# Cross-attention scores laid out by key: chunk maxima on VectorE, turned and spread as equal columns on TensorE

## The chip, the cores and the metric

The kernel runs on one core of a Trainium2 chip. The metric is the device time of one execution in microseconds (us). Before the change it is 1261.9 us, the median of three runs (1261.23, 1261.9, 1263.66). All operands are float32.

The engines are named as the profile names them: PE is TensorE's matmul stream and PEld its weight loads, DVE is VectorE, ACT is ScalarE, POOL is GpSimd, SP is SyncE, which only issues DMAs.

## The reference

One decoder layer on `x` (32 batches, 112 queries, 256 features) with a context of 375 keys in each batch: windowed self-attention, cross-attention, and a mixture of 8 experts (two for each token), each behind a layer norm and added to `x`. The change touches the cross-attention alone (16 heads of 16 features):

```
q = (hidden_states @ Wq).reshape(B, S, H, D).transpose(0, 2, 1, 3)
kv = (key_value_states @ Wkv).reshape(B, K, 2, H, D)
...
scores = jnp.einsum('bhsd,bhkd->bhsk', q, k)
rel = jnp.arange(K)[None, :] - jnp.arange(S)[:, None]
bias = rel_bias[_relative_position_bucket(rel)].transpose(2, 0, 1)[None]
scores = scores + bias
attn = jax.nn.softmax(scores, axis=-1)
out = jnp.einsum('bhsk,bhkd->bshd', attn, v).reshape(B, S, E)
return out @ Wo
```

A softmax over 375 keys thus needs, for each of 112 queries and 16 heads, the largest score, the exponentials of what lies below it, their sum, and the product with `v`. The sum comes out of that product: `v` carries a column of ones.

## The kernel before

**Slots.** The attention part is a list of slots, written out by hand and walked in the loop at L1226. A slot handles four heads (one in each 32-row strip of PE's array) of one batch: a cross item (g, b, s), from slot 20 to slot 147, and a self item two groups ahead, up to slot 119. Slots 0 to 18 hold self items only. Batches come in 8 groups of 4, so a group's cross items fill 16 slots. PE, DVE and ACT run in exactly the order in which the loop issues their instructions (`tc.manual_schedule(engines=IN_ORDER)`), and `pool_order` (L121) ties POOL's instructions to the same order.

**One slot.** The loop issues, in this order:

1. `scores` (L464). PE writes four banks `sc`, one for each strip: cross scores with queries on 112 partitions and 375 keys along the row (L477), and beside them self scores (L488). For each strip DVE adds the bias (or the mask), negates, stores `w`, and finds the row's least (L503, one instruction with its accumulator read). POOL then takes the least off `w` (L509): 4 x 375 elements for cross, 4 x 112 for self.
2. `average` (L533), in every second slot, for items three and four slots back: PE multiplies weights with `v` (L554), ACT copies the result (L558).
3. `weigh` (L515) for the item of two slots back: PE transposes `w` chunk by chunk, three chunks of 125 keys for cross and one of 112 for self, four heads each (L530), and ACT takes the exponential of each chunk into `wT`, with keys on the partitions (L531). Two of the chunks stand first, the others between the steps of 4.
4. Steps of the slot: projections of queries, keys and values (L383, L416, L450), context loads (L434), transposes of normed rows (L377).
5. Late steps: `divide` (L562), `turn` (L580), `attended` (L589) with its residual adds on DVE (L602), statistics of the layer norms (L343, L344), routing (L623 to L718), with small steps that go from DVE to POOL and back (L643 to L650, L676 to L678).

PE's order matters: the next slot's `scores` stand behind all of this slot's work on PE. The four `sc` banks serve one slot, so the next slot's cross scores wait for L503 on the bank. The transposes of `weigh` wait for POOL's L509, two slots earlier.

**The bias** (L288) is a table with queries on 112 partitions, all heads and 375 keys, spread by one DMA from a table by relative position (L298). The keys of the context come reversed from the host, so that the position runs the same way along both.

**After the attention** the expert part takes over (L1061): it starts while the last slots run, and is bound by PE and DMA. Its code isn't touched.

Of the kernel before, what the change touches and what calls it, by code (L numbers as in the profile page):

```python
# [11 lines left out]
F32 = mybir.dt.float32  # L12
# [26 lines left out]
NWARM = 24  # L39
LAG = 4  # L40
# [10 lines left out]
IN_ORDER = {mybir.EngineType.PE, mybir.EngineType.DVE, mybir.EngineType.Activation}  # L51
# [27 lines left out]
def decoder_kernel(  # L79
# [95 lines left out]
    with ExitStack() as att, ExitStack() as own_att:  # L175
# [112 lines left out]
        bias = wpool.tile([S, H, K], F32, name="bias")  # L288

        def spread_bias():  # L290

            vps = ps_pj.tile([P, 512], F32, tag="pj", name="vps")
            nc.tensor.matmul(vps[:H, :NREL], rb, hot, start=True, stop=True)
            by_rel = two.tile([H, NREL], F32, tag="ct", name="by_rel")
            nc.vector.tensor_copy(by_rel, vps[:H, :NREL])
            by_rel_d = dram.tile([H, NREL], F32, name="by_rel_d")
            nc.sync.dma_start(by_rel_d, by_rel)
            nc.sync.dma_start(  # L298
                bias,
                bass.AP(  # L300
                    tensor=by_rel_d.tensor, offset=by_rel_d.offset,
                    ap=[[1, S], [NREL, H], [1, K]],
                ),
            )
# [120 lines left out]
        def cross_queries(g, c):  # L425
            if c == 0:
                cross_q[g] = two.tile([P, NC2, 2, GT], F32, tag="q_cross", name=f"q_cross{g}")
            ps = ps_pj.tile([P, GT], F32, tag="pj", name=f"q2ps{g}_{c}")
            project(ps, wq_sb[:, :, c * P:(c + 1) * P], normed[g, 2][1])
            by_parity(cross_q[g][:, c], ps, g == 0)  # L430
# [32 lines left out]

        def scores(cross, selfs):  # L464

            name = "_".join(str(v) for part in (cross or (), *selfs) for v in part)
            w = two.tile([S, 4, K + S], F32, tag="w", name=f"w{name}", bufs=3)
            low = small.tile([S, 3, 4], F32, tag="low", name=f"low{name}")
            at = K if cross else 0
            sc = [ps_sc.tile([S, 512], F32, tag="sc", name=f"sc{name}_{r}") for r in range(4)]  # L470
            if cross:
                g, b, s = cross
                c, p = divmod(s, 2)
                kT, q = keys[g, b][1], cross_q[g]
                for r in range(4):
                    rows = slice(32 * r, 32 * r + 32)
                    scored[cross] = nc.tensor.matmul(  # L477
                        sc[r][:, :K], q[rows, c, p, b * S:(b + 1) * S], kT[rows, c, :],
                        start=True, stop=True,
                    ).ins  # L480
            if selfs:
                g, b, s = selfs[0]
                c, p = divmod(s, 2)
                n, at_b = len(selfs), slice(b * S, (b + 1) * S)
                q, k = self_in[g, c]
                for r in range(4):
                    rows = slice(32 * r, 32 * r + 32)
                    nc.tensor.matmul(  # L488
                        sc[r][:, at:at + n * S].rearrange("q (p k) -> q p k", p=n),
                        q[rows, at_b], k[rows, p:p + n, at_b], start=True, stop=True,  # L490
                    )
            spans = []
            if cross:
                spans.append((0, K))
            spans += [(at + i * S, at + (i + 1) * S) for i in range(len(selfs))]
            for r in range(4):
                for i, (lo, hi) in enumerate(spans):
                    if cross and i == 0:
                        c, p = divmod(cross[2], 2)
                        add = bias[:, 8 * c + 2 * r + p, :]  # L500
                    else:
                        add = wmask
                    nc.vector.tensor_tensor_reduce(  # L503
                        out=w[:, r, lo:hi], in0=sc[r][:, lo:hi], in1=add,
                        scale=-1.0, scalar=FAR, op0=ALU.add, op1=ALU.min,
                        accum_out=low[:, i, r:r + 1],
                    )
            for i, (lo, hi) in enumerate(spans):
                nc.gpsimd.tensor_tensor(  # L509
                    w[:, :, lo:hi], w[:, :, lo:hi],  # L510
                    low[:, i].unsqueeze(2).to_broadcast([S, 4, hi - lo]), op=ALU.subtract,
                )
            return w

        def weigh(cross, selfs, j, w):  # L515

            n = NKC if cross else 0
            if j == 0:
                name = "_".join(str(v) for part in (cross or (), *selfs) for v in part)
                wT = two.tile([KC, NKC + 1, 4, S], F32, tag="wT", name=f"wT{name}", bufs=3)  # L520
                if cross:
                    turned["c", *cross] = wT, 0
                for i, part in enumerate(selfs):
                    turned["s", *part] = wT, n + i
            wT, _ = turned[("c", *cross) if cross else ("s", *selfs[0])]
            lo, m = (j * KC, KC) if j < n else (n * KC + (j - n) * S, S)
            kind = "c" if j < n else "s"
            tp = ps_tr.tile([KC, 4, S], F32, tag="tr", name=f"{kind}tr{wT.name}_{j}")
            for r in range(4):
                nc.tensor.transpose(tp[:m, r, :], w[:, r, lo:lo + m], ident[:S, :S])  # L530
            nc.scalar.activation(wT[:m, j], tp[:m], AF.Exp, scale=-1.0)  # L531

        def average(half, cross, own):  # L533
# [9 lines left out]
            for i, (k, (g, b)) in enumerate(sides):  # L543
                for p in range(2):
                    wT, first = turned.pop((k, g, b, 2 * half + p))
                    n = NKC if k == "c" else 1
                    for j in range(n):
                        for r in range(4):
                            h = 8 * half + 2 * r + p
                            if k == "c":  # L550
                                v, x = v_cross[b % 2][:, j, h, :], wT[:, j, r, :]
                            else:
                                v, x = v_self[:, b, h, :], wT[:S, first, r, :]
                            nc.tensor.matmul(  # L554
                                av[32 * r:32 * r + 32, i, p, :], v, x,
                                start=(j == 0), stop=(j == n - 1),
                            )
# [660 lines left out]
        with tc.manual_schedule(engines=IN_ORDER):  # L1218
# [7 lines left out]
            for slot in range(min(steps), max(steps) + 1):  # L1226
# [12 lines left out]
                if slot in plan_at:  # L1239
                    planning = plan_at[slot]()  # L1240
                if slot in items:
                    made[slot] = scores(*items[slot])
                parts = []
                if slot - 2 in items:
                    cross, selfs = items[slot - 2]
                    w = made.pop(slot - 2)
                    n = NKC * bool(cross) + len(selfs)
                    parts = [partial(weigh, cross, selfs, j, w) for j in range(n)]
# [3 lines left out]
                for half in range(2):  # L1252
                    if sides := averages.get((slot, half)):
                        do(partial(average, half, sides.get("c"), sides.get("s")))
                for part in parts[:2]:
# [69 lines left out]
```

## Time and profile before

| what | value |
|---|---|
| median of three runs | 1261.9 us |
| the profiled execution | 1270.7 us, span 1269.0 us |
| self-attention slots alone | 0 to 84.8 us |
| cross and self slots (24 to 119) | about 105 to 739 us |
| cross slots alone (120 to 147) | 739 to 884 us |
| passage to the experts, experts | 884 to 1269 us |

How to read it: the page gives busy times of each engine, and the chain of work that ended last. Matmuls are pipelined, so the busy time of PE says little about its pace; the distance between the starts of two instructions of one kind says more. A row of groups has the line, the engine, the operation, what it writes and reads with shapes, the number of instructions, and after the bar the busy time with the mean of one in ns, then the engine's idle time just before them with what ended it. In a table by stage the columns after the stage are its length, the busy time and number of instructions of PE, PEld, DVE, ACT and POOL, PE's granted clock, the DMA engines' share and GB/s. In a list of waits the numbers are us in total, times, and the longest. In a timeline they are the start and the length in us, with the number of records merged; a float32 matmul leaves two records, a transpose one.

### The profile page before, as it was taken

Reading aid. Unit: us, or ns where it says so; the run is one execution under the profiler, and the core shown is the slowest. Engines: PE = TensorE matmul, PEld = TensorE weight load, DVE = VectorE, ACT = ScalarE, POOL = GpSimd, SP = SyncE. Lnnn points to the kernel's source line nnn. Section 1 sums busy time; section 2 is a strip of 40 time slices with the busy share of each in tenths; the row PEclk is TensorE's granted clock in tenths of the full one; section 3 lists DMA queues with packets and bytes.
Section 4 is the critical chain, followed back from the end, with each engine's and each line's share of the span. In section 5 each row is a group of like instructions: output and inputs, shape, how many; then the busy total and the mean of one; then the engine's idle time right before and its main releaser. Section 6 shows DMA issues by size and latency. Waiting matters only on the chain.

```text
span 1269.0 us, 29648 instructions
## 1 busy us (share of the span) xinstructions
PE 1227.4 (97%) x11648; PEld 972.5 (77%) x11648; DVE 651.0 (51%) x3012; ACT 570.1 (45%) x1201; POOL 839.0 (66%) x784
## 2 busy tenths in 40 slices
PE   9999999999999999999999999998789999999997
PEld 6666776777787787778778777766678898888886
DVE  5653654665566566557566665665325323332221
ACT  4454554555556456555555545454222222222222
POOL 8545664577767777767776796687556655665552
PEclk9999999999999999999999999999889999999999
DMA  8129876731100200200110020130366778888882
GB/s 229 34 69 197 203 169 161 180 87 42 44 26 14 73 14 14 74 24 15 39 33 26 14 59 26 36 128 25 115 209 195 212 208 276 239 234 244 244 247 30
DMA packets 70204, 143.00 MB, mean 113 GB/s; under 512 B 5521, under 2 KB 60498, under 8 KB 65074
## 3 DMA queue, kind: packets, MB, share of 16 engines
q0 software_dynamic: 20784, 85.92, 23.1%
q1 hardware_dynamic: 49282, 55.20, 17.3%
q8 instruction: 92, 1.51, 0.5%
q14 instruction: 46, 0.38, 0.1%
HBM read 90.88 MB, written 50.21 MB: 111 GB/s over the span
## 4 chain that ended last, share of the span: by engine, by line
PE 92%; ACT 2%; DVE 2%; POOL 1%; issue 1%; another core or an unknown queue 1%; DMA 0%; POOLq 0%; ACTq 0%; DVEq 0%
PE gu L1018 18%; PE wT L530 14%; PE py L1037 9%; PE sc L477 8%; PE k2ps L383 6%; PE v2ps L450 6%; PE avc_s L554 6%; PE ops L597 4%; PE ctrwT L530 3%; PE sc L488 3%; PE vps L416 2%; PE qps L383 2%; PE q2ps L383 2%; PE kps L383 2%; PE tp L377 1%; ACT wT L531 1%
## 5 line engine op out<-in xcount | busy, mean ns | idle before, releaser
L509 POOL TENSOR_TENSOR w<-w,low 112x448 f32<-112x448 f32 (+1 forms) x256 | 459.4, 1814 | 211.1 <-DVE low L503 210.1
L503 DVE CUSTOM_DVE_ANT_0 w<-sc,bias 112x375 f32<-112x375 f32 x512 | 270.4, 542 | 118.2 <-PE sc L488 96.2
L531 ACT ACTIVATE wT<-wT 125x448 f32<-125x448 f32 (+1 forms) x394 | 199.0, 542 | 100.7 <-PE wT L530 94.3
L1018 PE MATMUL gu<-xT,w 128*128 128x256 f32 (+1 forms) x1248 | 229.9, 342 | 1.9 <-issue 1.9
L530 PEld LDWEIGHTS wT<-ident,w 112*125 112x125 f32 (+1 forms) x1576 | 187.6, 174 | 46.1 <-issue 14.2
L1018 PEld LDWEIGHTS gu<-xT,w 128*128 128x128 f32 x1248 | 202.1, 192 | 26.8 <-issue 5.7
L530 PE MATMUL wT<-ident,w 112*125 112x112 f32 (+1 forms) x1576 | 216.0, 275 | 5.8 <-ACT wT L531 5.8
L1026 DVE SCALAR_TENSOR_TENSOR hid<-gu,w,sil 128x256 f32<-128x256 f32 (+1 forms) x156 | 67.2, 432 | 233.6 <-ACT sil L1023 228.2
L1044 POOL DMA_INDIRECT out_dram<-y,to x63 | 100.4, 1594 | 111.8 <-ACT y L1043 94.2
L1023 ACT ACTIVATE sil<-gu,w 128x256 f32<-128x256 f32 (+1 forms) x156 | 67.5, 433 | 147.4 <-PE gu L1018 131.9
L503 DVE CUSTOM_DVE_ANT_0 w<-sc,wmask 112x112 f32<-112x112 f32 x512 | 129.0, 268 | 2.6 <-PE sc L488 2.6
L477 PE MATMUL sc<-kT,q_cross 32*112 32x375 f32 x1024 | 123.3, 518 | 1.3 <-DVE low L503 1.0
L1037 PE MATMUL py<-w,hid 128*128 128x256 f32 x504 | 116.8, 383 | 0.4 <-DVE x L767 0.4
L1037 PEld LDWEIGHTS py<-w,hid 128*128 128x128 f32 x504 | 94.0, 193 | 12.1 <-DVE x L767 0.6
L450 PE MATMUL v2ps<-wkv_sb,ct 128*125 128x256 f32 x384 | 94.3, 381 | 0.0
L383 PE MATMUL k2ps<-ct,wkv_sb 128*128 128x375 f32 x256 | 92.3, 483 | 0.0
L503 DVE DVE_READ_ACCUMULATOR2_ANT low<- 112x1 f32 x1024 | 84.0, 82 | 0.0
L602 DVE TENSOR_TENSOR x<-x,ops 112x256 f32<-112x256 f32 x64 | 24.8, 418 | 111.1 <-PE ops L597 110.9
L1043 ACT ACTIVATE y<-py,gate 128x256 f32<-128x256 f32 x63 | 27.2, 471 | 108.6 <-PE py L1037 106.8
L725 POOL DMA_INDIRECT xslots<-xn,to x64 | 61.8, 966 | 19.7 <-issue 14.8
L962 POOL DMA_INDIRECT xg<-xslots,rows_i x63 | 60.7, 963 | 18.9 <-issue 17.4
L450 PEld LDWEIGHTS v2ps<-wkv_sb,ct 128*125 128x125 f32 x384 | 67.2, 188 | 7.7 <-DVE q_cross L389 0.5
(208 smaller groups left out, 1646.6 us busy)
## 6 DMA issues: line engine op xcount, KB each, us to landing
xslots<-zeros SPq DMA_DIRECT2D x28, 1060.0 KB, 7.6
ct<-in_ctx_t_dram SPq DMA_DIRECT2D x32, 375.0 KB, 3.3
x<-in_x_dram SPq DMA_DIRECT2D x8, 448.0 KB, 6.6
out_dram<-x SPq DMA_DIRECT2D x8, 448.0 KB, 3.2
bias<-by_rel_d SPq DMA_DIRECT2D x1, 2625.0 KB
xslots<-xn,to POOLq DMA_INDIRECT x64
xg<-xslots,rows_i POOLq DMA_INDIRECT x63
out_dram<-y,to POOLq DMA_INDIRECT x63
```

Source lines behind the costliest of these rows:

```text
L383: nc.tensor.matmul(ps, w[:, k, :], xT[:, k, :], start=(k == 0), stop=(k == NC2 - 1))
L450: nc.tensor.matmul(ps[:, i, :], ct[:, k, j * KC:(j + 1) * KC], wkv_sb[:, k, D:2 * D], start=(k == 0), stop=(k == NC2 - 1),)
L477: scored[cross] = nc.tensor.matmul(sc[r][:, :K], q[rows, c, p, b * S:(b + 1) * S], kT[rows, c, :], start=True, stop=True,).ins
L503: nc.vector.tensor_tensor_reduce(out=w[:, r, lo:hi], in0=sc[r][:, lo:hi], in1=add, scale=-1.0, scalar=FAR, op0=ALU.add, op1=ALU.min, accum ...
L509: nc.gpsimd.tensor_tensor(w[:, :, lo:hi], w[:, :, lo:hi], low[:, i].unsqueeze(2).to_broadcast([S, 4, hi - lo]), op=ALU.subtract,)
L530: nc.tensor.transpose(tp[:m, r, :], w[:, r, lo:lo + m], ident[:S, :S])
L531: nc.scalar.activation(wT[:m, j], tp[:m], AF.Exp, scale=-1.0)
L554: nc.tensor.matmul(av[32 * r:32 * r + 32, i, p, :], v, x, start=(j == 0), stop=(j == n - 1),)
L1018: nc.tensor.matmul(ps[:, m, :st], w[:, lo:lo + P], xT[:, c, :st], start=(c == 0), stop=(c == NC2 - 1),)
L1023: nc.scalar.activation(sil[:, :st], ps[:, 0, :st], AF.Silu, bias=w[:, bias_at + f:bias_at + f + 1])
L1037: nc.tensor.matmul(py[:, h, :], hid[:, f, h * P:(h + 1) * P], w[:, lo:lo + D], start=(f == 0), stop=(f == NFC - 1),)
L1044: added = nc.gpsimd.indirect_dma_start(out=out, out_offset=row_of(to[:, h:h + 1]), in_=y[:, h, :], in_offset=None, compute_op=ALU.add,)
```

## The change

Cross scores are made with keys on the partitions from the start. For each strip PE now makes three blocks of 125 keys x 112 queries, with the keys as the stationary operand. DVE adds a bias that is laid out the same way (125 partitions, 3 chunks, 112 queries) and stores `t`. The largest score of each query is found in two steps: DVE takes the largest over the three chunks (`most`, 125 x 448, reading the chunk index innermost). In the next slot, ahead of its scores, PE turns `most` (4 transposes) and DVE takes the largest along the row (`top`, one value for each query and head). PE then transposes `top` as a column repeated 125 times, which puts the value of every query on all 125 partitions; ACT copies this to `spread`, and POOL subtracts it from `t`. One slot later a single ACT instruction takes the exponential of all 1344 elements in place, and `average` reads `t` where it read `wT`. The transposes of cross weights and their three exponentials are gone; self items keep theirs. `t` has 6 buffers, shared with self-only slots; the tile of cross queries is split in two with one buffer each. The diff, cut to its core:

```diff
-        bias = wpool.tile([S, H, K], F32, name="bias")
+        bias = wpool.tile([KC, H, NKC, KC], F32, name="bias")
...
+            n = (NKC - 1) * KC + S
             nc.sync.dma_start(
-                bias,
+                bias.rearrange("k h j q -> k h (j q)")[:, :, :n],
                 bass.AP(
                     tensor=by_rel_d.tensor, offset=by_rel_d.offset,
-                    ap=[[1, S], [NREL, H], [1, K]],
+                    ap=[[1, KC], [NREL, H], [1, n]],
...
         def scores(cross, selfs):
...
-                for r in range(4):
-                    rows = slice(32 * r, 32 * r + 32)
-                    scored[cross] = nc.tensor.matmul(
-                        sc[r][:, :K], q[rows, c, p, b * S:(b + 1) * S], kT[rows, c, :],
-                        start=True, stop=True,
-                    ).ins
+                for j in range(NKC):
+                    for r in range(4):
+                        rows = slice(32 * r, 32 * r + 32)
+                        scored[cross] = nc.tensor.matmul(
+                            sc[r][:KC, j * S:(j + 1) * S], kT[rows, c, j * KC:(j + 1) * KC],
+                            q[rows, p, b * S:(b + 1) * S], start=True, stop=True,
+                        ).ins
...
             for r in range(4):
+                if cross:
+                    c, p = divmod(cross[2], 2)
+                    nc.vector.tensor_tensor(
+                        t[:, r], sc[r][:KC, :at].rearrange("k (j q) -> k j q", j=NKC),
+                        bias[:, 8 * c + 2 * r + p, :, :S], op=ALU.add,
+                    )
...
+            if cross:
+                most = two.tile([KC, 4, S], F32, tag="most", name=f"most{name}")
+                nc.vector.tensor_reduce(most, t.rearrange("k r j q -> k r q j"), AX.X, ALU.max)
+                shown[cross] = t, most
+            return (w, low) if selfs else None
+
+        def maxima(cross):
+            t, most = shown[cross]
...
+            for r in range(4):
+                nc.tensor.transpose(turned_most[:, r, :], most[:, r, :], ident[:KC, :KC])
+            top = small.tile([S, 4], F32, tag="top_w", name=f"top_w{name}")
+            nc.vector.tensor_reduce(top, turned_most, AX.X, ALU.max)
+            shown[cross] = t, top
+
+        def lessen(cross):
+            t, top = shown[cross]
...
+            for r in range(4):
+                nc.tensor.transpose(
+                    by_key[:, r, :], top[:, r:r + 1].to_broadcast([S, KC]), ident[:S, :S]
+                )
+            spread = two.tile([KC, 4, S], F32, tag="spread", name=f"spread{name}")
+            nc.scalar.copy(spread, by_key)
+            nc.gpsimd.tensor_tensor(
+                t, t, spread.unsqueeze(2).to_broadcast([KC, 4, NKC, S]), op=ALU.subtract
+            )
...
+        def exps(cross):
+            t, _ = shown.pop(cross)
+            t = t.rearrange("k r j q -> k (r j q)")
+            nc.scalar.activation(t, t, AF.Exp)
...
+                prior, prior2 = (items.get(slot - i, (None,))[0] for i in (1, 2))
+                if prior:
+                    do(partial(maxima, prior))
                 if slot in items:
                     made[slot] = scores(*items[slot])
...
                 for half in range(2):
                     if sides := averages.get((slot, half)):
                         do(partial(average, half, sides.get("c"), sides.get("s")))
+                if prior:
+                    do(partial(lessen, prior))
+                if prior2:
+                    do(partial(exps, prior2))
+                if slot in items and made[slot]:
+                    do(partial(lessen_own, len(items[slot][1]), *made[slot]))
```

## The prediction

> **What bounds the kernel now.** The page comes first: busy times, then the chain that ended last.
>
> ```profile
> PE 1227.4 (97%) x11648; PEld 972.5 (77%) x11648; DVE 651.0 (51%) x3012; ACT 570.1 (45%) x1201; POOL 839.0 (66%) x784
> ...
> PE 92%; ACT 2%; DVE 2%; POOL 1%; issue 1%; another core or an unknown queue 1%; DMA 0%; POOLq 0%; ACTq 0%; DVEq 0%
> ```
>
> TensorE (PE) is the bound: 92% of the chain. The changed code runs in the 128 cross-attention slots, 84.8 to 884 us. Next, the stage table for slots 24 to 119 (cross and self together), then the same stretch's waits, of PE and of VectorE (DVE):
>
> ```profile
> 112.00:737.00 625.00, 615.50 (x7180) 477.56 (x7179) 377.51 (x1874) 338.10 (x697) 438.84 (x375) 1.00 0.26 68
> ```
>
> ```profile
> PE qps L383 <- DVE x L767: 3.1, 4, 0.8
> PE lg L626 <- ACT lT L620: 1.1, 3, 0.4
> ...
> PE sc L477 <- DVE low L503: 0.7, 1, 0.7
> ```
>
> ```profile
> DVE w L503 <- PE sc L488: 93.5, 48, 5.5
> DVE x L602 <- PE ops L597: 91.8, 29, 7.0
> DVE tot L678 <- POOL tot L677: 31.1, 7, 5.5
> DVE gt L650 <- POOL pr L643: 18.5, 7, 2.7
> ```
>
> PE is busy 615.5 of 625 us at clock 1.00 and hardly waits for VectorE; VectorE waits for PE. That freedom comes from distance: PE reads a slot's weights two slots later. Last, groups by shape (300 to 700 us) and PE's timeline of one short slot:
>
> ```profile
> L503 DVE CUSTOM_DVE_ANT_0 w<-sc,bias 112x375 f32<-112x375 f32 x243 | 131.8, 542 | 50.0 <-PE sc L488 45.3 <-issue 4.5
> L530 PE MATMUL wT<-ident,w 112*125 112x112 f32 x728 | 103.9, 279 | 0.0
> L664 DVE TENSOR_REDUCE rank<-gt 112x32 f32<-112x256 f32 x3 | 1.2, 414 | 0.0
> L602 DVE TENSOR_TENSOR x<-x,ops 112x256 f32<-112x256 f32 x32 | 12.0, 417 | 54.3 <-PE ops L597 54.3
> ```
>
> ```profile
> 579.57 0.90 PE L477 MATMUL sc<-kT,q_cross 32*112 32x375 f32 x8
> 580.29 0.37 PE L488 MATMUL sc<-k_self,q_self 32*112 32x112 f32 x8
> 580.59 1.13 PE L530 MATMUL wT<-ident,w 112*125 112x112 f32 x8
> 581.55 1.90 PE L450 MATMUL v2ps<-wkv_sb,ct 128*125 128x256 f32 x8
> 583.29 0.97 PE L530 MATMUL wT<-ident,w 112*125 112x112 f32 x8
> 584.20 0.90 PE L477 MATMUL sc<-kT,q_cross 32*112 32x375 f32 x8
> ```
>
> From L477 to the next L477 this slot lasts 4.63 us. Slots alternate: even ones hold an average (1.6 us) and more, odd ones none. In slots 76 to 91 (454.9 to 560.8 us, a pattern that recurs every 16) the even slots last 7.17, 6.67, 7.17, 7.36, 7.36, 10.94, 10.19, 8.00 (64.86) and the odd 4.94, 4.63, 4.93, 6.50, 4.93, 4.63, 4.17, 6.36 (41.09): 105.95 us.
>
> **PE's part: 0.51 us a slot removed.** Matmul records overlap, so I use distance from start to start. L530's transposes of 125 columns start every 0.109 us in the timeline. Gone: 12 per slot, 1.31 us. New: 4 of the maxima and 4 of the equal columns, 8 x 0.109 = 0.87. The cross scores took 0.72 (579.57 to 580.29). Now three chunks, in two records each (as L488), make 6 groups of four row strips; a group of L488 with 112 columns takes 0.096, with 125 I take the transposes' 0.109: 0.65. Together 1.31 + 0.72 - 0.87 - 0.65 = 0.51; were VectorE free, 128 x 0.51 = 65 us.
>
> **VectorE's part: 1.9 us a slot added.** Per strip, L503's pair (375 and 112 elements) starts every 0.67 us in the timeline, the 112 part taking 0.19; four make 2.6. The add replacing the 375 has 336 elements. Its nearest row is L602 (scores' kind of operands, one from PSUM): 417 ns for 256, started 0.34 apart, so 336 x 1.04 + 0.07 = 0.42. Four strips: 4 x (0.42 + 0.195) = 2.46. The maximum over chunks reads 1344 elements: L664's 414 ns for 256 is 1.04 ns an element and 0.15 fixed, so 1.55. The maximum of the turned maxima (500 elements): 0.67, or 0.58 to the next start. VectorE goes from 377.5 / 96 = 3.9 to 5.8 us a slot, against PE's 6.5 - 0.5 = 6.0. On average that still fits; but it is in-order on both sides now.
>
> **Strided reading, the unknown price.** The maximum over chunks takes elements 448 bytes apart, one after another; no large row does this. One end is 1.04 ns an element (L664, dense). The reciprocals L573 read every 32nd element: 253 ns for 16, 354 for 32, so 6.3 ns each; but the dense 4 of L678 (178 ns) lie on that line, so I give that pace to the division. As the other end I take the slowest elementwise pace from SBUF here, POOL's L656 (730 ns for 256 against 240 for 32 of L681): 2.19 ns, so 3.09 us. I choose 1.04, VectorE's own row. [...] No run so far shows which.
>
> **The new wait.** PE's first instruction of a slot is now the turning of the previous slot's maxima, and behind it in order stands everything of the slot. The shortest slot is thus a loop: turning 0.44, scores until VectorE can start 1.04 (0.65 + own 0.12 + 0.27 to a matmul's end), four strips 2.46, maximum 1.55, release 0.06 (L767's first end to PE's next start): **5.55 us**. The second transposes wait for VectorE's 0.67, which lies beside the scores if VectorE is free. It isn't after a slot with residual adds and statistics (L602, L343): those adds wait for PE's last matmul, run 0.68 + 0.88 us, so the turned maximum starts 1.7 us into the slot instead of 0.6, and the loop is 1.7 + 0.58 + 2.46 + 1.55 + 0.06 = **6.35 us**. I count the slot after L678's wait for POOL so too.
>
> **The sum.** Even slots keep their own bound: 64.86 - 8 x 0.51 = 60.8. Odd ones take the larger of their time less 0.51 and the loop: four at 6.35 (77, 81, 83, 89), three at 5.55 (79, 85, 87), one at 5.85 (91): 47.9. Together 108.7 against 105.95: +2.7, six such groups +16.4 us. Cross-only slots 120 to 146 (139.8 us) have loops of 0.44 + 0.92 + 4 x 0.42 + 1.55 + 0.06 = 4.65, or 5.45 after statistics, 6.4 in the planning slot 135: evens 85.1 to 78.9, odds 54.7 to 66.1, +5.2. Slots 20 to 23: +1.5. The last item has no cover: 1.68 + 1.55 + 0.5 + 0.72 + 0.5 + 0.53 + 3.1 + 1.42 = 10.0 from scores to weights, against 1.9 + 2.7 + 0.5 + 1.7 = 6.8: +3.2. **Sum +26 us**. The profiled execution took 1270.7 (span 1269.0), so it would take 1297; the median of the runs is 1261.9, 0.7% lower, and I add the sum there: **1288 us**.
>
> **Costs put at nothing, and their cover.** POOL's subtraction reads two whole operands: 1344 x 2.19 + 0.17 = 3.1 us for L509's 2.69 (1.67 ns an element would make 2.4); POOL goes from 4.6 to 5.0 us of a slot over 6. Its result is needed a slot later, so PE doesn't feel it until POOL is full. ScalarE: three exponentials of 542 ns become one of 1344 elements (0.84 ns each by L454's 372 and 587 ns, 1.3 to 1.4) and a copy of 0.53: +0.3 of a slot, from 54% to 59% busy. The larger bias load issues at 22.6 us in SP's queue, its first reader starts at 86.6. No DMA moves past another. Experts after 940 us and self-only slots before 84.8 keep their instructions.
>
> **Rivals.**
> - *Strided maximum* at 2.19 ns: loops grow by 1.54. Evens 63.1, odds 60.0: +17.1 a group, 103 in all; cross-only slots +35, edges +11: +149, **1411 us**. [...]
> - *VectorE blocked by POOL*: L650 and L678 wait 22.2 and 31.5 us over 8 groups now, hidden. If PE feels them whole (less the 0.8 counted at 83): (2.8 + 3.9 - 0.8) x 8 = +47 on the loops, about 60 with POOL's longer subtraction: **1335 us**.
> - *Faster: the loop fits the short slots.* PE's 0.51 is real in every slot whose loop is shorter. The odd slots break even if they sum to 45.2 instead of 47.9, a plain loop of 5.2. Without fixed costs on VectorE (336 and 112 elements at 1.04 make 0.35 and 0.12, the maximum 1.40) the loop is 4.8 and 5.6: odds 42.7, -2.5 a group, -15, cross-only -5, edges +3: **1245 us**. For it: VectorE's instructions overlap their ends (0.42 busy, 0.34 apart); against: the starts used already hold that.
>
> **How the numbers follow.** Forecast 0.46 (1268 to 1312 by itself), strided 0.24, POOL 0.14, faster 0.16. What this kernel's measurement can tell from no change is about 0.2% (2.5 us). Between the faster case and the forecast lies 0.04 for no change, taken from the forecast; slower 0.80, faster 0.16. The range 1250 to 1415 leaves out half of the faster case and those strided or blocked times that exceed 1415.
>
> **What would show it.** PE's mean gain: cross-score groups 0.65 us, transposes 0.109 apart. Maximum over chunks 1.55 us: right; near 3: strided rival. PE idle before the maxima's transposes in odd slots, about 1 us each, released by the maximum over chunks: the loop. Idle before the equal columns' transposes after slots with residual adds: the late maximum. Odd slots near 4.1 us would prove me wrong.

## The result, and the profile after

The changed kernel takes **1364.6 us** (median of four runs, 1362.1 to 1367.1) against 1262.8 for the kernel before beside it: ratio 1.0805, 95% interval 1.0773 to 1.0837. The change costs 102 us; the prediction said 26. The profiled execution took 1362.3 us (span 1360.6).

The page of the changed kernel, busy times and chain:

```profile
PE 1210.7 (89%) x13184; PEld 965.2 (71%) x13184; DVE 907.2 (67%) x2756; ACT 594.5 (44%) x1073; POOL 885.6 (65%) x784
...
PE 67%; DVE 15%; POOL 7%; ACT 6%; issue 5%; DMA 0%; POOLq 0%; ACTq 0%; DVEq 0%
```

PE has 17 us less to do than before (1227.4), and its share of the chain falls from 92% to 67%. VectorE, POOL and ScalarE, together 5% before, now hold 28%. The stretch of the cross and self slots, and PE's longest waits in it:

```profile
112.00:800.00 688.00, 600.45 (x8283) 466.09 (x8287) 563.76 (x1685) 353.80 (x601) 472.12 (x373) 0.98 0.26 64
```

```profile
PE mtr L534 <- DVE most L523: 33.6, 22, 2.4
PE btr L546 <- DVE top_w L536: 30.4, 26, 2.3
PE tp L382 <- ACT kT L447: 10.4, 16, 0.7
PE ops L649 <- ACT v_cross L458: 5.7, 5, 1.1
```

PE idles 88 of 688 us, where it idled 9.5 of 625. Two waits make most of it: the maxima's transposes wait for the maximum over chunks, the equal columns for the largest of the turned maxima. The next two are for ScalarE's copies of keys and values.

What the new instructions cost, by groups of the page:

```profile
L551 POOL TENSOR_TENSOR t<-t,spread 125x1344 f32<-125x1344 f32 x128 | 390.0, 3047 | 261.8 <-ACT spread L550 251.0
L510 DVE TENSOR_TENSOR t<-sc,bias 125x336 f32<-125x336 f32 x512 | 249.2, 503 | 23.0 <-PE sc L503 18.9
L523 DVE TENSOR_REDUCE most<-t 125x448 f32<-125x1344 f32 x128 | 216.5, 1691 | 1.1
L565 ACT ACTIVATE t<-t 125x1344 f32<-125x1344 f32 x128 | 170.1, 1329 | 1.8 <-POOL t L551 1.7
L536 DVE TENSOR_REDUCE top_w<-mtr 112x4 f32<-112x500 f32 x128 | 85.0, 664 | 32.4 <-PE mtr L534 30.7
```

Single instructions came out almost as predicted (3.1 us; 0.42 from the start of an add to the start of what follows it, which overlaps the row's 0.50; 1.55; 1.3 to 1.4; 0.67); the waits did not. The loop can be read in one short slot of PE, slot 79:

```profile
512.58 0.59 PE L534 MATMUL mtr<-ident,most 125*112 125x125 f32 x4
513.10 0.92 PE L491 MATMUL sc<-q_cross,kT 32*125 32x112 f32 x24
513.85 0.38 PE L503 MATMUL sc<-k_self,q_self 32*112 32x112 f32 x8
514.15 0.69 PE L546 MATMUL btr<-ident,top_w 112*125 112x112 f32 x4
...
515.06 1.90 PE L454 MATMUL v2ps<-wkv_sb,ct 128*125 128x256 f32 x8
518.51 0.61 PE L534 MATMUL mtr<-ident,most 125*112 125x125 f32 x4 [1.55 <-DVE most L523]
```

PE is done after 4.4 us and waits 1.55 us. On VectorE the first strip starts at 514.24, the maximum at 516.67: turning 0.52, scores 1.14, strips 2.43, maximum 1.69, release 0.15, together **5.93 us** where the prediction had 5.55. After slots with residual adds the slot takes 6.79 instead of 6.35. In slot 77, where PE turns the maxima from 498.84 us on, VectorE's late work holds the rest of the chain:

```profile
500.79 0.65 DVE L536 TENSOR_REDUCE top_w<-mtr 112x4 f32<-112x500 f32 x1
...
503.77 1.70 DVE L523 TENSOR_REDUCE most<-t 125x448 f32<-125x1344 f32 x1
```

The largest starts 1.95 us into the slot (forecast 1.7), the strips follow 0.56 later and take 2.42, then the maximum 1.70 and the release 0.15: **6.78 us**.

The dearest slot of each group is number 83. VectorE's timeline, then POOL's, then PE's:

```profile
539.37 0.13 DVE L728 TENSOR_REDUCE tot<-pr 112x4 f32<-112x32 f32 x1
542.02 0.18 DVE L730 RECIPROCAL tot<-tot 112x4 f32<-112x4 f32 x1 [2.52 <-POOL tot L729]
542.11 0.65 DVE L536 TENSOR_REDUCE top_w<-mtr 112x4 f32<-112x500 f32 x1
```

```profile
536.72 3.05 POOL L551 TENSOR_TENSOR t<-t,spread 125x1344 f32<-125x1344 f32 x1 [0.49 <-ACT spread L550]
...
540.62 1.06 POOL L626 TENSOR_TENSOR by_q<-by_q,tot_av 128x512 f32<-128x512 f32 x1
541.76 0.23 POOL L729 TENSOR_SCALAR tot<-tot 112x4 f32<-112x4 f32 x1
```

```profile
542.90 0.95 PE L546 MATMUL btr<-ident,top_w 112*125 112x112 f32 x4 [2.26 <-DVE top_w L536]
...
544.39 2.96 PE L454 MATMUL v2ps<-wkv_sb,ct 128*125 128x256 f32 x8
```

VectorE waits 2.5 us for a small POOL instruction that stands behind POOL's long ones. PE, in want of the turned maximum, idles 2.3 us; then its clock is granted at half for 3.4 us, so `v2ps` takes 2.96 us instead of 1.90. The slot takes 10.1 us; the prediction gave it 6.35.

Group by group (from first cross score to first cross score, us):

| slots | before | after | PE's work alone (e10) | loop, nothing taken off (e11) |
|---|---|---|---|---|
| 28 to 43 | 108.9 | 108.6 | 95.0 | 108.5 |
| 60 to 75 | 105.9 | 120.1 | 101.6 | 114.1 |
| 76 to 91 | 105.9 | 119.0 | 101.7 | 115.6 |
| 120 to 131 | 64.1 | 70.2 | 59.0 | 68.7 |
| 132 to 146 | 75.8 | 90.1 | 65.9 | 87.4 |

The last two columns are experiments told below. The group without routing steps (28 to 43) loses nothing on balance: the loop takes 13.5 us there too (95.0 to 108.5), but PE's own work is 13.9 us shorter. Each group of 16 with routing steps loses 13 to 15 us.

### The profile page after: what moved, and what is told of

Read it like the earlier page. It is cut to its first block, busy times and chain, and to the rows that moved or that the text cites. A ratio compares the mean times of both kernels' runs of the same rounds, so it can differ in the third digit from the quotient of the medians.

```text
span 1360.6 us, 32519 instructions
## 1 busy us (share of the span) xinstructions
PE 1210.7 (89%) x13184; PEld 965.2 (71%) x13184; DVE 907.2 (67%) x2756; ACT 594.5 (44%) x1073; POOL 885.6 (65%) x784
## 4 chain that ended last, share of the span: by engine, by line
PE 67%; DVE 15%; POOL 7%; ACT 6%; issue 5%; DMA 0%; POOLq 0%; ACTq 0%; DVEq 0%
PE gu L1070 16%; PE py L1089 8%; PE avc_s L606 5%; PE sc L491 5%; PE btr L546 4%; PE v2ps L454 4%; DVE t L510 4%; DVE most L523 4%; PE mtr L534 3%; POOL t L551 3%; PE ops L649 3%; ACT t L565 3%; PE str L582 2%; PE vps L421 2%; PE qps L388 2%
## 5 line engine op out<-in xcount | busy, mean ns | idle before, releaser
L551 POOL TENSOR_TENSOR t<-t,spread 125x1344 f32<-125x1344 f32 x128 | 390.0, 3047 | 261.8 <-ACT spread L550 251.0
L510 DVE TENSOR_TENSOR t<-sc,bias 125x336 f32<-125x336 f32 x512 | 249.2, 503 | 23.0 <-PE sc L503 18.9
L523 DVE TENSOR_REDUCE most<-t 125x448 f32<-125x1344 f32 x128 | 216.5, 1691 | 1.1
L565 ACT ACTIVATE t<-t 125x1344 f32<-125x1344 f32 x128 | 170.1, 1329 | 1.8 <-POOL t L551 1.7
L546 PE MATMUL btr<-ident,top_w 112*125 112x112 f32 x512 | 90.9, 302 | 46.9 <-DVE top_w L536 46.8
L534 PE MATMUL mtr<-ident,most 125*112 125x125 f32 x512 | 79.1, 278 | 54.2 <-DVE most L523 51.5
L491 PE MATMUL sc<-q_cross,kT 32*125 32x112 f32 x3072 | 120.3, 286 | 0.0
L546 PEld LDWEIGHTS btr<-ident,top_w 112*125 112x125 f32 x512 | 68.5, 194 | 67.7 <-issue 46.6
L491 PEld LDWEIGHTS sc<-q_cross,kT 32*125 32x125 f32 x3072 | 97.2, 186 | 22.4 <-issue 22.4
L536 DVE TENSOR_REDUCE top_w<-mtr 112x4 f32<-112x500 f32 x128 | 85.0, 664 | 32.4 <-PE mtr L534 30.7
```

Source lines behind the costliest of these rows:

```text
L491: scored[cross] = nc.tensor.matmul(sc[r][:KC, j * S:(j + 1) * S], kT[rows, c, j * KC:(j + 1) * KC], q[rows, p, b * S:(b + 1) * S], start=T ...
L510: nc.vector.tensor_tensor(t[:, r], sc[r][:KC, :at].rearrange("k (j q) -> k j q", j=NKC), bias[:, 8 * c + 2 * r + p, :, :S], op=ALU.add,)
L523: nc.vector.tensor_reduce(most, t.rearrange("k r j q -> k r q j"), AX.X, ALU.max)
L534: nc.tensor.transpose(turned_most[:, r, :], most[:, r, :], ident[:KC, :KC])
L546: nc.tensor.transpose(by_key[:, r, :], top[:, r:r + 1].to_broadcast([S, KC]), ident[:S, :S])
L551: nc.gpsimd.tensor_tensor(t, t, spread.unsqueeze(2).to_broadcast([KC, 4, NKC, S]), op=ALU.subtract)
```

## The experiments

The first theory: **the loop** (scores, VectorE's strips, maximum, turning, in order on both engines) sets the short slots, and VectorE now hands its own waits on to PE. Rivals: **PE's own work** did not shrink; the **strided maximum**; **POOL and ScalarE** stand in the way. The runs were made on more than one chip, and the kernel before took 1261 us on some and 1273 on others; so each figure is a ratio to the kernel before on the same chip. The ratio doesn't take the chip away entirely (see e1): differences of less than about 0.01 between runs of different chips decide nothing here.

**e1_recip.** The gates' reciprocal leaves VectorE:

```diff
-            nc.vector.reciprocal(tot2, tot2)
+            nc.gpsimd.tensor_tensor(tot2, tot2, negone, op=ALU.pow)
```

> Edit: the reciprocal of the gates' sums (L730), for which VectorE waits 2.5 us behind POOL's long subtractions once in every group of 16 slots, is made on POOL. Loop theory (VectorE, in order, passes each of its own waits on to PE): slot 83 falls from 10.04 to about 6.8 us, slot 84 from 8.4 to about 7; 3.3 to 4.8 us in each of seven groups, 1331 to 1341 us in place of 1364, and the granted clock no longer falls to 0.5 near 543 us. Rival, PE's own work (PE was not made shorter by the change): 1364 as before, since PE's instructions are the same.

Measured 1.0703 (1.0679 to 1.0727). Slot 83 falls from 10.07 to 6.10 us, as expected, and the half clock there is gone (the mean granted clock is 0.977, 0.969 in the changed kernel). The whole gains 0.010, about half of what was expected (0.018 to 0.026): slot 90 grows from 7.15 to 8.75 (in the changed kernel slot 74, its like, takes 8.75 already), and slots 86 and 88 by 1.2 and 1.6 us. The last two seem to be of the chip: there PE pauses 0.3 to 0.4 us between single matmuls of the averages ("issue"), also in the old kernel's layout on another chip where that kernel takes 1273 us (11.98 and 11.54 us in e15 against 10.94 and 10.19). What makes the pauses isn't known. So VectorE does hand POOL's delay on to PE, but this one place in each group is worth about 1%.

**e2_fill.** Needless transposes where PE idles:

```diff
+            if slot_of["c", *cross] + 1 in idle_m:
+                for r in range(9):
+                    nc.tensor.transpose(
+                        turned_most[:, r % 4, :], ident[:KC, :S], ident[:KC, :KC]
+                    )
```

> Edit: nine needless transposes (0.98 us by 0.109 each) are put ahead of the maxima's transposes in 22 slots and ahead of the equal columns in 25 slots, in which PE idles there by the trace. They add 46 us of work to PE and nothing to anyone else. Loop theory: PE waits in these places anyway, so the time stays within 8 us of 1364; if the half clock comes from PE's idle stretches, it is even lower by up to 15. Rival, PE's own work: 1364 + 46 = 1410.

Measured 1.0763 (1.0735 to 1.0790): 46 us of added work cost nothing. Between 112 and 800 us of the filled kernel:

```profile
112.00:800.00 688.00, 635.50 (x8681) 497.44 (x8679) 565.12 (x1689) 352.65 (x601) 473.43 (x375) 1.00 0.26 64
```

PE is busy 35 us longer, and the granted clock is 1.00 instead of 0.98. In the changed kernel nine stretches at half clock (34 us in all) lie between 100 and 890 us; here one. So the idle stretches brought on most of the half clock: with them filled, eight of the nine are gone. Where it came on top of a wait, as in slots 67, 83 and 99, it cost 1.75 us (10.07 to 8.32). All nine stretches together, 34 us at half speed, can't have cost more than 17 us (an estimate), and pauses in slots 86 and 88 as in e1 hide it in the total.

**e3_first.** The maximum over chunks left out:

```diff
-                nc.vector.tensor_reduce(most, t.rearrange("k r j q -> k r q j"), AX.X, ALU.max)
-                shown[cross] = t, most
+                shown[cross] = t, t[:, :, 0, :]
```

> Leaves out the maximum over chunks: the first chunk alone gives the value that is taken off. Loop theory: the plain loop falls by 1.69 us from 5.95 to 4.26, under PE's own time, so PE's waits ahead of the maxima's transposes (48 us) go, those ahead of the equal columns (47 us) mostly stay, since they come from adds and statistics: 1305 to 1320 us. Strided-maximum theory in its strong form (a price of 3.09) is out already by the 1.69 us measured. Rival, PE's own work: 1355 to 1364.

Measured 1.0406 (1.0381 to 1.0432), 50 us less, in the expected range: PE's wait for `most` is gone, the one for `top_w` stays (38.2 us from 112 to 800 us, 30.4 in the changed kernel). Slots 79 and 87 take 4.22 us against 4.63 before and 5.95 after.

**e4_late.** The maxima are turned at the end of the next slot, all that follows one slot later:

```diff
-                if prior:
-                    do(partial(maxima, prior))
...
-                if prior:
-                    do(partial(lessen, prior))
                 if prior2:
-                    do(partial(exps, prior2))
+                    do(partial(lessen, prior2))
+                if prior3:
+                    do(partial(exps, prior3))
...
+                if prior:
+                    do(partial(maxima, prior))
                 for fn in late.get(slot, []):
```

> Edit: the maxima are turned at the end of the next slot's work on PE instead of at its beginning, the equal columns and the exponentials come one slot later, the averages too (four and five slots after the item). No work is added or left out. Loop theory: no instruction of PE waits for VectorE's latest result any more; the 95 us of waits ahead of the two kinds of transposes go, and the half-clock stretches with them: 1255 to 1280, and with the 0.5 us a slot that PE was to save, 1210 to 1240. Rival, PE's own work: PE is full at once and not shorter than before, 1330 or more. Rival, VectorE and POOL are full (5.9 and 5.6 us a slot of work against 6.0): 1290 to 1340, with VectorE without idle time in the slots with adds.

Measured 1.0525 (1.0507 to 1.0543): the loop theory's figure was missed by far; 1.0525 of 1262.8 is 1329 us, in the range of the rival by which VectorE and POOL are full. The old waits are gone (3.9 us are left before the equal columns), but a new one came, before the scores, for the bank that VectorE hasn't read: 22.4 us in five places, up to 4.5. VectorE and POOL ahead of the scores of slot 81:

```profile
491.35 0.18 DVE L694 RECIPROCAL tot<-tot 112x4 f32<-112x4 f32 x1
492.64 3.22 DVE L702 TENSOR_TENSOR gt<-pr 112x256 f32<-112x256 f32 x1 [1.11 <-POOL pr L695]
```

```profile
492.37 0.24 POOL L695 TENSOR_TENSOR pr<-pr,tot 112x32 f32<-112x32 f32 x1
492.56 3.02 POOL L551 TENSOR_TENSOR t<-t,spread 125x1344 f32<-125x1344 f32 x1
```

The comparison L702 takes 0.42 us in the kernel before, in the changed one and in e1 and e3. Here it takes 3.22 in seven of eight groups, starting 0.08 us after POOL's subtraction and ending 0.28 after it.

**e8_late_gt.** e4 with POOL's next work tied behind the comparisons:

```diff
-            for i, fn in enumerate((choose, rank, front, gate, weight_gates, count, address)):
-                put_late(norm_t_at + 1 + i, fn, g)
+                if fn is rank:
+                    put_late(norm_t_at + 1 + i, front, g)
```

> The late maxima with one edit: front directly behind rank, so that no POOL subtraction runs beside VectorE's comparison L702, which took 3.22 us in seven of eight groups beside a subtraction of 3.02 us and 0.42 us in all other kernels. If the two engines shut each other out: L702 back at 0.42 us, slot 81 from 13.4 to 6 or 7 us, the half clock behind it gone, six to seven times: ratio 1.015 to 1.03 in place of 1.0525. If L702's length is only waiting that the trace books wrongly: 1.05.

Measured 1.0267 (1.0229 to 1.0305), and L702 is back at 0.42 us:

```profile
L702 DVE TENSOR_TENSOR gt<-pr 112x256 f32<-112x256 f32 x8 | 3.4, 425 | 10.6 <-POOL pr L695 10.6
```

So it was POOL's subtraction that held the comparison up: 3.22 us beside it, 0.42 without it, and the time is 0.026 less (on another chip). The subtraction itself was not longer for it (3.02 us, 3.05 in the changed kernel). Slot 81 did not fall to 6 or 7 us, however, but stayed at 13.2 with a half clock (its 48 cross matmuls of the average took 2.47 us, 1.36 in slot 79); the group gains 5.8 us (slots 76 to 91: 118.3 to 112.5), half of it in slot 80, whose length holds the wait for the bank (7.91 to 5.12), half in slot 86 (12.45 to 9.61), whose cause isn't known.

**e5_late_mend** adds to e8 the reciprocal of e1 and puts the 1.33 us exponential behind the slot's other work on ScalarE.

```diff
-                if prior3:
-                    do(partial(exps, prior3))
...
+                if prior3:
+                    do(partial(exps, prior3))
                 if prior:
                     do(partial(maxima, prior))
                 for fn in late.get(slot, []):
```

> Three mends on top of the late maxima (e4_late: 1.0525 of before): the gates' reciprocal on POOL; front (two POOL instructions of 0.73 us) directly behind rank, so that POOL waits for VectorE's comparisons instead of starting its 3.0 us subtraction beside them; the exponential of 1.33 us behind the slot's other ScalarE work, so that PE's waits for kT (11 us) go. Loop theory with VectorE's stalls: the 4.5 us wait ahead of the cross scores in slot 81 of every group goes with the half clock behind it (7 us of 8 groups), kT's waits go: ratio 0.99 to 1.02. Rival, VectorE is full (5.9 us of work a slot): 1.03 to 1.05.

Measured 1.0303 (1.0270 to 1.0336), no better than e8 and outside the loop theory's range; it lies in that of the rival, a full VectorE, which e6 then contradicts. The wait for `kT` falls to 3.7 us, and other waits for ScalarE's copy of the columns (7.3 us) and exponential (4.3 us) take its place.

**e6_late_first** is e5 with the first chunk alone, as in e3.

> The same three mends and the late maxima, and the maximum over chunks left out (the first chunk alone gives the value that is taken off). VectorE falls from 5.9 to 4.2 us a slot. Loop theory: PE is the bound in every slot and shows what the change saves it: odd slots 79 and 87 took 4.22 us with the first chunk against 4.63 before, 0.41 us a slot, 52 us of 128: ratio 0.96 to 0.98. Rival, PE's own work is no shorter: 1.00 or more.

Measured 1.0227 (1.0191 to 1.0262): a miss. VectorE is busy 55% instead of 69%, and hardly anything is gained. So VectorE's amount of work isn't what holds the late versions. The figure lies in the rival's range too, but e10 finds PE's work shorter. What of it could be read: the later averages wait 0.3 us each for the exponential, the scores of three slots in a group still stretch to 2.0 to 2.8 us instead of 0.9 (in slots 77, 81 and 85), and slot 81 of each group has a stretch at half clock (at 485 us the 48 cross matmuls of the average took 2.47 us, 1.36 in slot 79). Why these versions stay at 1.02 is not settled.

**e7_no_shift.** Maximum, turning, columns and subtraction all left out, the exponential of the raw scores:

```diff
-                if prior:
-                    do(partial(maxima, prior))
...
-                if prior:
-                    do(partial(lessen, prior))
```

> The changed kernel without maximum, its turning, equal columns, copy and subtraction: the exponential is taken of the raw scores, nothing guards against overflow. What is left of the change is the layout by key alone. Loop theory: PE loses 12 transposes a slot (1.31 us) and the loop is gone, PE bounds: 128 x 1.29 = 165 us less than before, ratio 0.86 to 0.89. Rival, the layout itself costs (cross scores with keys stationary, averages): 0.92 or more.

Measured 0.8954 (0.8922 to 0.8985), just above the expected range. Odd slots lose 1.32 us where nothing else waits (79: 3.31 us). The layout by key without any maximum is worth 132 us; finding and spreading the maximum costs 234.

**e10_turns.** e7 with the eight transposes put back, of a constant:

```diff
+                nc.tensor.transpose(tp[:m, r * n:(r + 1) * n], ident[:n, :m], ident[:n, :n])
```

> As e7_no_shift (0.8954), with the eight transposes of the change put back into PE's order at their places, but of a constant: nobody waits for their result and they wait for nothing. It separates PE's work from the waits: e7_no_shift and the changed kernel lie 0.185 (234 us) apart. By 0.131 us a transpose in the trace the work is 1.05 us a slot, 134 us; where PE waited for ScalarE in e7_no_shift it now covers (up to 0.4 us in 11 of 16 slots, 35 us). Both causes matter: 0.97 to 1.005. PE's work alone explains the slowdown: 1.05 to 1.08. The waits alone explain it: below 0.93.

Measured **0.9507** (0.9486 to 0.9527), between the ranges "the waits alone" and "both": the eight transposes cost 70 us net. PE without waits would have won 62 us against the kernel before. So PE's own work doesn't explain any of the slowdown.

**e11_unused.** The changed kernel without the copy to `spread` and POOL's subtraction:

```diff
-            nc.scalar.copy(spread, by_key)
-            nc.gpsimd.tensor_tensor(
-                t, t, spread.unsqueeze(2).to_broadcast([KC, 4, NKC, S]), op=ALU.subtract
-            )
```

> The changed kernel (1.0805), with maximum, turning, largest and equal columns as they are, but ScalarE's copy of the columns and POOL's subtraction of 3.05 us left out, so nothing is taken off the scores. It separates the loop between PE and VectorE from POOL. Loop theory: the loop stands, only POOL's part in slots 83 and 84 of every group (4 us, eight groups) and the half clock there go: 1.04 to 1.06. POOL in the way (it holds VectorE, and VectorE PE): as with the bare transposes, 0.97 to 1.01.

Measured **1.0508** (1.0482 to 1.0533): the loop theory's figure. Slots 79 and 87 stay at 5.95 us, 77, 81 and 89 at 6.79; slot 83 falls to 7.31, 84 to 7.70. PE's waits:

```profile
PE mtr L534 <- DVE most L523: 42.0, 36, 2.4
PE btr L546 <- DVE top_w L536: 25.4, 27, 1.4
```

The loop stands by itself, without POOL's subtraction.

**e13_only_top and e14_only_max** split the loop. Both are e11; e13 turns the first chunk, as e3 does, and e14 has

```diff
-                nc.tensor.transpose(
-                    by_key[:, r, :], top[:, r:r + 1].to_broadcast([S, KC]), ident[:S, :S]
-                )
+                nc.tensor.transpose(by_key[:, r, :], ident[:S, :KC], ident[:S, :S])
```

> As e11_unused (nothing is copied or taken off the scores), and without the maximum over chunks: the first chunk is turned. Of the loop only PE's wait for the largest of the turned maxima is left, behind VectorE's adds and statistics. Bare transposes are at 0.951, the whole loop at 1.051. If the late largest is the greater half: 1.00 to 1.02. If the maximum over chunks is: 0.96 to 0.99.

> As e11_unused, but the equal columns are transposes of a constant, so PE does not wait for the largest of the turned maxima. Of the loop only PE's wait for the maximum over chunks is left: odd slots at 5.95 us instead of 5.95 to 7.3, some 4 us in each of seven groups: 1.02 to 1.035 if the two waits are mostly apart; if the late largest was the cause of most, 0.97 to 1.00.

Measured 0.9929 (0.9897 to 0.9960) and 1.0584 (1.0553 to 1.0615). The first lies between its two ranges. Without the maximum over chunks 0.058 of the loop's 0.100 is gone (slots 79 and 87 at 4.22 us, as in e10, 77 and 81 at 6.06): the maximum is the greater half. Without PE's wait for the largest nothing is gained (slots 76 to 91 take 115.8 us, 115.6 in e11): slots 77, 81 and 89 stay at 6.8 us, and PE waits for `most` instead:

```profile
PE mtr L534 <- DVE most L523: 52.2, 36, 2.4
PE str L575 <- DVE top_w L536: 8.1, 16, 0.9
```

That is where both of e14's expectations went wrong: VectorE's late work delays its strips, and so the maximum over chunks, whether or not PE waits for the largest as well.

**e16_dense.** The same maximum without strides:

```diff
-                nc.vector.tensor_reduce(most, t.rearrange("k r j q -> k r q j"), AX.X, ALU.max)
+                nc.vector.tensor_reduce(
+                    most.rearrange("k r q -> k (r q)"),
+                    t.rearrange("k r j q -> k (r j q)").rearrange("k (m i) -> k m i", i=NKC),
+                    AX.X, ALU.max,
+                )
```

> The changed kernel with the maximum over groups of three neighbouring elements instead of over the three chunks (another value is taken off, which changes nothing in the result short of overflow): same numbers of elements, no strides. If the stride costs: 1.55 us by the pace of the small dense reduction, 0.14 us in some 50 slots, 1.073 to 1.081. If 1.69 us is what 1344 elements take: no change, and 1.69 in the trace.

```profile
L523 DVE TENSOR_REDUCE most<-t 125x448 f32<-125x1344 f32 x128 | 198.3, 1549 | 1.1
```

1.55 us dense, 1.69 strided. Slot 79 shrinks by just this, 5.95 to 5.81; the whole, at 1.0856 (1.0824 to 1.0887), lies above both expectations and shows no gain, with slot 86 at 14.7 us, pauses as under e1 among it.

**e12_shared.** e8 with one maximum for the four heads of a slot:

```diff
-                nc.vector.tensor_reduce(most, t.rearrange("k r j q -> k r q j"), AX.X, ALU.max)
+                nc.vector.tensor_reduce(most, t.rearrange("k r j q -> k q (r j)"), AX.X, ALU.max)
```

> On top of e8_late_gt (1.0267): one value for the four heads of a slot, the largest of all twelve chunks, so PE turns one block of maxima and one of equal columns instead of four each, VectorE's second maximum reads 125 elements instead of 500, ScalarE copies 112 instead of 448. The value taken off is at least each head's largest, so nothing overflows; the result is the same as long as a head's largest lies less than 87 below that of its three neighbours. Loop theory with PE full: six transposes of 0.131 us a slot go, 0.79 x 128 = 101 us: ratio 0.94 to 0.965. Rival, VectorE is the bound (5.4 us of work a slot): 0.99 to 1.02.

Measured 1.0396 (1.0370 to 1.0422): slower than e8, against both expectations. What neither had foreseen stands in one group:

```profile
L523 DVE TENSOR_REDUCE most<-t 125x112 f32<-125x1344 f32 x110 | 273.1, 2483 | 0.5
```

The same 1344 elements with the same step of 448 bytes, but twelve in a row of steps instead of three: 2.48 us instead of 1.69. VectorE gets 0.4 us a slot more to do, not less. PE's waits for VectorE (60 to 900 us) rise from 23 us in e8 to 77, and the granted clock falls from 0.975 to 0.944 on average. That the longer maximum is the whole cause is not shown: e6 took 1.5 us a slot off VectorE and gained little.

**e9_clamp.** e7 with another guard against overflow, in the instruction that adds the bias:

```diff
-                    nc.vector.tensor_tensor(
-                        t[:, r], sc[r][:KC, :at].rearrange("k (j q) -> k j q", j=NKC),
-                        bias[:, 8 * c + 2 * r + p, :, :S], op=ALU.add,
+                    nc.vector.scalar_tensor_tensor(
+                        t[:, r], sc[r][:KC, :at].rearrange("k (j q) -> k j q", j=NKC), 80.0,
+                        bias[:, 8 * c + 2 * r + p, :, :S], op0=ALU.min, op1=ALU.add,
```

> As e7_no_shift, with another guard: the instruction that adds the bias first takes the smaller of score and 80 (one instruction as before). It gives the reference's softmax as long as no score leaves the range from -80 to 80, and no overflow ever; nothing is subtracted. Layout theory: as e7_no_shift, ratio 0.890 to 0.900. Rival, the second operation makes the strips slower than 0.50 us and PE waits for the banks: 0.905 to 0.93.

Measured **0.8962** (0.8915 to 0.9009): 1127.6 us, 10% under the kernel before and 17% under the changed one. The second operation is free (501 ns a strip against 500 in e7). It computes the reference's softmax only while the scores lie between -80 and 80, which a user has to know of the data.

**e15_old_bare.** Is that gain the layout's, or that of leaving the shift out? The kernel before without its subtraction for cross scores:

```diff
             for i, (lo, hi) in enumerate(spans):
+                if cross and i == 0:
+                    continue
```

> The kernel before, with POOL's subtraction left out for the cross scores (the exponential is taken of the raw scores; the row's least is still found, in the same instruction). Layout theory: PE is the bound there and POOL hidden, so 0.985 to 1.002, and the 0.895 of e7_no_shift is the gain of the layout by key. Rival, leaving out the shift is what gains: 0.93 or less.

Measured 1.0135 (1.0097 to 1.0174): no gain, and a little above the layout theory's range. Why it loses a little stays open (its odd slots take what they took before; slots 86 and 88 hold the pauses named under e1). So what e7 and e9 win is the layout's, and the layout wins it only where no maximum is found and spread.

## Why the prediction was wrong

The direction was right, and so was the mechanism of the forecast; its size was a quarter of the truth. The time of 1364.6 lies in the range, but beyond the forecast's own 1268 to 1312. In ratios: PE's work -0.049 (e10), the loop +0.100 (e11 less e10), copy and subtraction +0.030 (after less e11): -62, +126 and +38 us, together the 102 measured. By place: slots 24 to 119 take 67 us more (forecast 16), the cross-only slots 120 to 146 20 (5), slots 20 to 23 6 (1.5).

- **PE's part, 65 us if VectorE were free**: 62 by e10. That the sum came out right was luck: two errors cancel. A block of four transposes takes 0.525 us, not 0.44, and the cross scores 0.74, not 0.65: in slots 76 to 91 PE won 4.2 us, not 8.2. The pace inside a block was right (0.105 to 0.111 a transpose, 0.109 a group of scores in slot 79); left out were longer steps of about 0.20 where, in most places, one kind of block follows another (in slot 79 the last transpose starts at 512.90, the first score at 513.10). But in slots 28 to 43 it won 13.9: there the old kernel's transposes took PE 33.0 us instead of 29.0, with 4.2 us of waits for ScalarE's exponentials besides, which I had not looked at.
- **Even slots keep their own bound**: in kind right for some (slots 76 and 82 take the same in e10 and after, 6.76 and 6.75, 6.93 and 6.93), but not in size. Those of 76 to 91 were forecast at 60.8 us and took 64.6. In e10 they take 62.6, so half of the miss is PE's 0.51, which was 0.28 there, and half is waits: 84 and 86 take 0.65 and 1.06 us more after than in e10.
- **Strided reading**: the choice of 1.55 was nearly right: the maximum took 1.69 us, and the stride costs 0.14 of it in this order of reading (1.55 dense, e16). In e12's order the same 1344 elements, with 112 results instead of 448, took 2.48, which is 0.93 more than dense; so the rival's worry was sound, and this pattern hardly meets it.
- **The new wait** is the first step that failed, by its size. Forecast 5.55 and 6.35, measured 5.93 and 6.79: turning +0.08, scores +0.10, maximum +0.14, release +0.09, strips -0.03; in the longer one the late start +0.25, maximum +0.15, release +0.09. Four terms of five were a little short, all in one chain. Over the kernel the forecast gave the loop 88 us (26 plus 65, less 3 for the tail); it cost 126. Some 12 of these 38 lie in slots 120 to 146 (forecast 5.2 + 27 x 0.51 = 19, e11 less e10 31), where the planning slot 135 took 9.3 us for 6.4. The path of the longer loop was right: its sum runs through VectorE's late work, the strips and the maximum, and in e14, where PE doesn't wait for the largest, these slots stay at 6.8 us.
- **Costs put at nothing** is the second. "PE doesn't feel it until POOL is full" held for POOL's own throughput (69% busy), not for VectorE, which stands behind POOL's 3.05 us when it needs a small result. Slot 83 was forecast at 6.35 and took 10.1, 1.75 of it by the half clock (e2); e1 brings it to 6.1. This was my rival of 0.14, at 47 to 60 us; it came true in part, beside the forecast: copy and subtraction cost 38 together. How these divide was not measured: e1, which takes VectorE's wait out of slot 83, is worth some 13, and ScalarE has a share (copy and exponential stand ahead of `kT`, and PE waits 0.65 us in three slots a group; without the copy, in e11, 0.2; I had called ScalarE hidden too).
- **Faster** did not happen. With nobody waiting (e10) the time is 0.951 of before, so what kept it away were the waits.
- What I said would show the loop did show it: PE idles 1.55 us before the maxima's transposes of slot 80, released by `most`. Equal columns idle 1.1 us after slots with adds.

## What to carry to other kernels

When an engine that was always ahead begins to wait for the result of the slot before, look at the loop's length, not at the average load: in slot 79 the loop took 5.93 us, while PE was done after 4.4. Add up every link from measured starts, and expect the sum to be short (5.55 here). An engine that is in order can hand a small wait on, as in slot 83, where VectorE's wait of 2.5 us for POOL became one of 2.3 us on PE: look for the long instructions that stand ahead of a short one whose result is awaited. A price of doing the work with nobody waiting (e10) and one of the waits without the last consumer (e11) split a slowdown cleanly.

## What the runs showed of the hardware

- After 2.3 us without work PE's granted clock was at half for 3.4 us (slot 83, 543.1 to 546.5 us); after 2.25 us, ended at 779.7 us, it stayed at 1.00. Of two waits of 1.78 us, one was followed by such a stretch (it ended at 477.4 us), the other not (598.0 us). With the gaps filled, one such stretch was left of nine (e2).
- VectorE's comparison of two SBUF operands took 3.22 us beside a POOL subtraction of 3.02 us, 0.42 otherwise (e4, e8). The strips' adds, which read one operand from PSUM, took 0.497 to 0.503 us on average in every run of the layout by key, and none more than 0.51 in the changed kernel.
- A maximum over 1344 elements took 1.55 us dense, 1.69 with three steps of 448 bytes to a result, 2.48 with twelve (e16, after, e12).
- A second elementwise operation in VectorE's add cost nothing: 501 against 500 ns (e9, e7).
- Four transposes in a block started 0.105 to 0.111 us apart, with 0.20 to the first score behind them (slot 79).
